# Activations of VectorE's channels half a slot later, and the cosine products inside convolution 1's multiply-adds

## The chip, the cores and the metric

The program runs on one core of a Trainium2 chip. The metric is the device time of one execution in microseconds (us), median of the runs. PE is TensorE, DVE is VectorE, ACT is ScalarE, POOL is GpSimd, SP is SyncE. Each takes its instructions in the order in which the program lists them; semaphores join them.

## The reference

The input x is 8 images of 32 channels, 128 x 128 pixels, f32. `_gn` is a group norm, `_conv` a plain convolution. Cut to what matters:

```python
xb = _patch_match_stack(x)            # per pixel the 8 best of 25 shifts: 256 channels
dct = _conv(xb, dct_w, groups=C)      # "cosine transform": 8 -> 8 in each of 32 groups
h = relu(_conv(_conv(xb, w1), w2, groups=CK, pad=1))   # convolution 1: pointwise, then 3x3 depthwise
h = relu(_conv(_conv(h, w3), w4, groups=CK, pad=1))    # convolution 2
wiener = sigmoid(_conv(_conv(h, w5), w6, groups=CK, pad=1))   # convolution 3
filt = _conv(wiener * dct, inv_dct_w, groups=C)
return _conv(filt, agg_w)
# whole: x = x + L0(_gn(x)); x = x + 5x5 convolution(_gn(x))     (layer 1)
```

## The kernel before

An image is cut into 17 strips of about 8 rows: 136 steps over all images. A step has four slots, numbered by `i` and run in the order 3, 2, 1, 0. Slots 3, 2 and 1 run convolutions 3, 2 and 1, each for another strip, so that a strip goes through convolution 1 in one step, 2 in the next and 3 in the one after; slot 0 ends a strip: the transform's products, the aggregation and the residual sum.

Of the 256 channels, 128 get their depthwise 3x3 on PE (`depthwise_t`, L751) and the other 128 on DVE (`depthwise_v`): one ACT copy with a scale for the first tap (L722) and eight `scalar_tensor_tensor` instructions (L725, "multiply-adds" here) into `acc{i}1`. The activation is an ACT instruction in place (L729 for DVE's channels, L764 for PE's channels). The pointwise products are L670 (`pv`, for DVE's channels) and L694 (`p`, for PE's). Both read the previous convolution's two halves, PE's half `src(0)` first, then DVE's half `src(1)`.

PE, DVE and ACT take their instructions in the order in which this Python code emits them (`manual_schedule`). POOL and SP, which issue DMAs, are ordered by the framework. So the loop over slots is the schedule. In it the generators of a slot are advanced in later places: `depthwise_v` stops at each `yield`. Of a slot's `new_v`, the first `next` emits the copy, the second the eight multiply-adds; the generator is then called `dv` in the next slot and `kept` in the one after.

In slot order, ACT's part of a slot is: the copies of `pv` into `tv` (L678), L722, the two selects of one gather (L616, L617), the copies of `p` into `t` (L701), the copy of the gathered pixels (L638), squares (L452, when there are some), L729, two more selects, two L764. PE's part is: `pv` (slots 3 to 1) or the transform `pc` (L810, slot 0), in slot 3 the aggregation `pa` (L831), then `p`, the gather `pg` (L631), and the depthwise `pw` of the slot before.

The preparation of the next image (differences, squares, the top 8) and layer 1 of the previous one stand in queues; DVE's "D" queue gives out some work in each slot (`tick`), after slot 0's products and before the next multiply-adds. `final_dct` (slot 0) multiplies `acc3` with the transform, four DVE instructions L818 that read PSUM tiles `pc`. In the slot after, `final_add` runs `pa` on PE and then the residual sum L839 on DVE, which frees `pa`'s tile. Layer 1's sum of its products is L936.

All these PSUM tiles (`pv`, `p`, `pg`, `pc`, `pa`, layer 1's `p5` and some small ones) come from one pool of five banks (`ps_x`). A new tile waits for the last reader of the tile that had its bank; which bank it gets is decided when the program is built.

`rows_before_v` moves two rows of `tv` by a DMA on SP (L655), which waits for the multiply-adds that read them.

Of the kernel before, what the change touches and what calls it, by code (L numbers as in the profile page):

```python
# [44 lines left out]
def bm3d_conv_preact(  # L45
# [165 lines left out]
    def push(task):  # L211
        want = next(task, None)
        if want:
            which, cost, *wait = want
            queues[which].append((cost, task, now[0] + (wait[0] if wait else 0)))
# [150 lines left out]
    def prep(b):  # L366

        xn = load_image(b, nc.gpsimd) if b else first
        yield "P", 0
        yield "D", 5.5  # L370
        st = work.tile([P, 8, 6], F32, name=f"st_{b}", tag="st")
        for i in range(8):
            nc.vector.bn_stats(
                st[:, i], xn[:, 3 + 4 * i : 7 + 4 * i, 2 : 2 + W]
            )
        mv = work.tile([P, 2], F32, name=f"mv_{b}", tag="mv")
        nc.vector.bn_aggr(mv, st.rearrange("p a b -> p (a b)"))
        yield "A", 0
        nc.scalar.copy(xn[:, :, 0:2], xn[:, :, 2:3].to_broadcast([P, HR, 2]))
        nc.scalar.copy(  # L380
            xn[:, :, 2 + W :], xn[:, :, 1 + W : 2 + W].to_broadcast([P, HR, 2])
        )
        mr = yield from group_stats(mv, f"a{b}")
        nc.vector.tensor_scalar(
            xn, xn, mr[:, 0:1], mr[:, 1:2], op0=ALU.subtract, op1=ALU.mult
        )
        push(sources(b, xn))

        idx = work.tile([P, 4, 8, K, 4], U32, name=f"idx_{b}", tag="idx", bufs=1)

        sq = dram.tile([NO // 2, 4, HR - 2, HX], F32, name=f"sq_{b}", tag="sq")
        for i in range((HR - 2) // SR):
            pd = ps_d.tile([P, SR // 2, HX], F32, name=f"pd_{b}_{i}", tag="pd")

            for aa in ((2, 4), (0, 0), (1, 1), (3, 2), (4, 3), (5, 5)):
                yield "D", PAIR
                push(squares(b, i, pd, xn, aa, sq, idx))
# [254 lines left out]
    def rows_before_v(i, b, n):  # L652
        v = tv[i - 1]
        if n < NS:
            nc.sync.dma_start(v[:, 0:2], v[:, R : R + 2])  # L655
        else:
            nc.gpsimd.memset(v[:, 0 : i + 1], 0.0)
# [53 lines left out]
    def depthwise_v(i, b, n):  # L711
        v = tv[i - 1]
        nr = R if n < NS else i
        out_ = accp.tile([P, R, W], F32, name=f"acc{i}_{b}_{n}_1", tag=f"acc{i}1")
        acc = out_[:, :nr]
        for k, (dy, dx) in enumerate(
            ((1, 1), (0, 0), (0, 1), (0, 2), (1, 0), (1, 2), (2, 0), (2, 1), (2, 2))
        ):
            tap = dwv[:, i - 1, 3 * dy + dx : 3 * dy + dx + 1]
            rows = v[:, dy : dy + nr, dx : dx + W]  # L720
            if k == 0:
                nc.scalar.activation(acc, rows, AF.Copy, scale=tap)  # L722
                yield out_
            else:
                nc.vector.scalar_tensor_tensor(  # L725
                    acc, rows, tap, acc, op0=ALU.mult, op1=ALU.add
                )
        yield
        nc.scalar.activation(acc, acc, funcs[i - 1])  # L729
        yield  # L730
        rows_before_v(i, b, n)

    def depthwise_t(i, b, n):
# [62 lines left out]
    def final_dct(b, n, acc, xf, j0, j1):  # L796

        for r0 in range(0, R, 4):
            a, z = max(r0, j0), min(r0 + 4, j1)
            if a >= z:  # L800
                continue


            pc = [
                ps_x.tile([P, 4, W], F32, name=f"pc_{b}_{n}_{m}_{r0}", tag="x") for m in range(2)
            ]
            for h in range(2):
                for m in range(2):
                    o = 64 * ((h + m + 1) % 2)
                    nc.tensor.matmul(  # L810
                        pc[m][o : o + 64, : z - a],
                        ldct[64 * h : 64 * h + 64, m],
                        xf[64 * h : 64 * h + 64, m, a:z],
                        start=True,
                        stop=True,
                    )
            for m in range(2):
                nc.vector.tensor_mul(acc[m][:, a:z], acc[m][:, a:z], pc[m][:, : z - a])  # L818
# [179 lines left out]
    def unit(stage, u, *rest):  # L998
        if 0 <= u < len(units) and units[u]:
            if stage is gather_load:  # L1000
                at = (units[u][0], units[u][1] % 8 // 2)
                until(lambda: at in ready, 4.0)
            stage(*units[u], *rest)
# [20 lines left out]
    def turn(credit):  # L1024
        now[0] += 1
        run("D", credit)
        run("A")
        run("P")
        run("Q")

    def until(cond, credit):
        while not cond():
            turn(credit)

    with tc.manual_schedule(engines=ORDERED):
        push(prep(0))
        push(weights())
        push(mixes())
        xbd[0] = dram.tile([P, 2, H, W], F32, name="xbd_0", tag="xbd")
        for i in range(3):  # L1040
            nc.gpsimd.memset(tb[i][0:64, 0], 0.0)
        for u in range(7):
            unit(gather_load, u)

            for _ in range({2: 3, 3: 1}.get(u, 0)):
                turn(4.0)
            unit(gather_select, u - 2)
            unit(gather_pixels, u - 3)
        u = 4

        dt = dv = kept = iter(())

        later = iter(())

        for s in range(len(steps) + 2):
            if s < len(steps):
                b, n = steps[s]
                if s == 2:
                    push(bands())
                if n == (0 if b else 4) and b + 1 < NB:  # L1060
                    until(lambda: b in ready, 4.0)
                    push(prep(b + 1))
                if n == NS - 1 and b + 1 < NB:
                    until(lambda: b + 1 in ready, 4.0)
                    xbd[b + 1] = dram.tile([P, 2, H, W], F32, name=f"xbd_{b+1}", tag="xbd")
            for i in (3, 2, 1, 0):
                si = s - (i - 1 if i else 2)
                live = 0 <= si < len(steps)
                new_v = new_t = iter(())
                if live:  # L1070
                    bi, ni = steps[si]

                if live and i:
                    src = source(i, bi, ni)
                    pointwise_v(i, bi, ni, lws[i - 1], src)
                    new_v, new_t = depthwise_v(i, bi, ni), depthwise_t(i, bi, ni)
                    accs[i, bi, ni] = [None, next(new_v)]
                next(later, None)
                if live and not i:
                    if ni == 0:  # L1080
                        x1d[bi] = dram.tile([C, H, W], F32, name=f"x1d_{bi}", tag="x1d")
                        stats[bi] = work.tile([P, NS + 1, 6], F32, name=f"stat_{bi}", tag="stat")
                    xr, xf, j0, j1 = fins.pop(si)
                run("P")
                if live and not i:
                    final_dct(bi, ni, accs[3, bi, ni], xf, j0, j1)

                run("Q")
                if s < len(steps):
                    unit(gather_select, u + 1, (0,))  # L1090
                    unit(gather_load, u + 3)
                    tick(b, i)
                next(later, None)
                next(new_v, None)
                if live and i:
                    pointwise_t(i, bi, ni, lws[i - 1], src)
                next(kept, None)
                if s < len(steps):
                    unit(gather_pixels, u)
                next(dt, None)  # L1100
                run("A")
                next(dv, None)
                if s < len(steps):
                    unit(gather_select, u + 1, (1,))
                    u += 1
                next(dt, None)
                kept, dv, dt = dv, new_v, new_t
                if live and not i:
                    later = end(bi, ni, xr, j0, j1)
                if not i and 0 <= s - 1 < len(steps):  # L1110
                    fins[s - 1] = final_load(*steps[s - 1])
        next(kept, None)
        for _ in later:
            pass
        until(lambda: {(NB - 1, 0), (NB - 1, 1)} <= done, 4.0)
# [62 lines left out]
```

## Time and profile before

| | |
|---|---|
| median of 3 runs | 6544.47 us (6539.76 to 6554.23) |
| the profiled execution, its own time | 6544.27 us |
| its span in the profile | 6542.5 us |
| PE busy | 6179.8 us (94%) |
| DVE busy | 5857.8 us (90%) |
| ACT busy | 5058.6 us (77%) |
| POOL busy | 3087.2 us (47%) |
| chain that ended last | PE 55%, DVE 26%, POOL 5%, ACT 5%, DMA 4%, issue 4% |

Busy time is the time in which an engine executed. "Idle before" is the time for which an engine stood still ahead of a group of instructions, and the arrow names what ended it. Line numbers are those of the kernel before. Times on a timeline count from the span's start. An image takes about 788 us of the span, and the stalls repeat with it.

### The profile page before, as it was taken

What the parts mean: (1) busy time and instruction counts of PE and PEld (TensorE: products, weight loads), DVE (VectorE), ACT (ScalarE), POOL (GpSimd) and SP (SyncE); (2) the same over time, 40 slices, a digit from 0 to 9 for tenths busy, and PEclk for the clock granted to TensorE, in tenths of its full rate; (3) what the DMA queues carried; (4) which work ended last, traced back from release to release, by engine and by line L of the source; (5) the groups of instructions that cost most, each with busy time, mean ns of one, the idle gap of its engine ahead of it and who ended that gap; (6) DMA issues with size and microseconds to landing.
All of it is one profiled execution on the core that took longest, in us unless ns stands there. A gap on an engine that the chain in (4) does not pass through costs nothing.

```text
span 6542.5 us, 234200 instructions
## 1 busy us (share of the span) xinstructions
PE 6179.8 (94%) x102306; PEld 3215.9 (49%) x102306; DVE 5857.8 (90%) x8828; ACT 5058.6 (77%) x6698; POOL 3087.2 (47%) x5015
## 2 busy tenths in 40 slices
PE   4799999999999999999999999999999999999997
PEld 1444445455554545545454544544545454455553
DVE  7899988999989999999989999889998999878776
ACT  5787769778787877887788787977869788787772
POOL 8345436444364444644446444554345544334334
PEclk8899999999999999999999999999999999999998
DMA  4555555555555555565556555555555555455553
GB/s 85 126 134 144 125 126 143 141 143 138 131 149 138 137 146 129 145 151 134 140 132 156 136 137 141 134 142 140 139 135 134 146 146 138 115 147 144 136 134 81
DMA packets 544960, 886.21 MB, mean 135 GB/s; under 512 B 248880, under 2 KB 312944, under 8 KB 543936
## 3 DMA queue, kind: packets, MB, share of 16 engines
q0 software_dynamic: 383648, 611.87, 37.3%
q1 hardware_dynamic: 157776, 258.11, 16.1%
q8 instruction: 805, 13.19, 0.9%
q10 hardware_dynamic: 2512, 1.25, 0.1%
q14 instruction: 219, 1.79, 0.1%
HBM read 420.60 MB, written 216.49 MB: 97 GB/s over the span
## 4 chain that ended last, share of the span: by engine, by line
PE 55%; DVE 26%; POOL 5%; ACT 5%; DMA 4%; issue 4%; SPq 0%; ACTq 0%; DVEq 0%; POOLq 0%
PE pw L751 18%; DVE acc L725 17%; PE pv L670 14%; PE p L694 13%; PE pg L631 4%; POOL xtd L424 3%; DVE idx L537 3%; PE pc L810 2%; DMA t<-t 2%; DVE df L444 1%; PE pd L459 1%; PE p L924 1%; PE pa L831 1%; DVE acc L818 1%; ACT df L452 1%
## 5 line engine op out<-in xcount | busy, mean ns | idle before, releaser
L725 DVE SCALAR_TENSOR_TENSOR acc<-tv,dwv,acc 128x1024 f32<-128x1024 f32 (+3 forms) x3264 | 4032.1, 1237 | 163.7 <-ACT acc L722 59.9
L751 PE MATMUL pw<-t,dwd 96*32 96x254 f32 (+7 forms) x31680 | 2113.2, 419 | 23.8 <-DMA t<-t 17.9
L751 PEld LDWEIGHTS pw<-t,dwd 96*32 96x32 f32 (+1 forms) x31680 | 1079.9, 110 | 850.1 <-issue 385.5
L616 ACT ACTIVATE sel<-ib,nplace 128x1024 f32<-128x1024 uint8 x1024 | 1170.6, 1143 | 62.3 <-DMA ib<-idxd 62.3
L617 ACT ACTIVATE sel<-sel 128x1024 f32<-128x1024 f32 x1024 | 1086.0, 1061 | 32.5
L670 PE MATMUL pv<-acc,lw 128*32 128x512 f32 x8448 | 964.3, 593 | 49.9 <-DVE acc L818 41.7
L694 PE MATMUL p<-acc,lw 128*32 128x256 f32 x16768 | 977.4, 380 | 19.4 <-DVE xy L936 19.4
L602 POOL DMA_DIRECT2D ib<-idxd x512 | 293.0, 572 | 1209.2 <-ACT sel L616 1099.4
L791 POOL DMA_DIRECT2D xf<-xbd x1088 | 653.6, 633 | 329.2 <-PE pc L810 187.1
L694 PEld LDWEIGHTS p<-acc,lw 128*32 128x32 f32 x16768 | 568.0, 111 | 411.2 <-issue 59.3
L678 ACT COPY tv<-pv 128x512 f32<-128x512 f32 (+2 forms) x784 | 437.0, 578 | 366.9 <-PE pv L670 358.8
L729 ACT ACTIVATE acc<-acc 128x1024 f32<-128x1024 f32 (+3 forms) x408 | 417.3, 1023 | 349.0 <-DVE acc L725 348.8
L631 PE MATMUL pg<-sel,xt 120*32 120x88 f32 (+1 forms) x24576 | 609.9, 245 | 56.6 <-ACT sel L617 56.2
L631 PEld LDWEIGHTS pg<-sel,xt 120*32 120x32 f32 x24576 | 559.3, 111 | 211.5 <-ACT sel L617 72.2
L670 PEld LDWEIGHTS pv<-acc,lw 128*32 128x32 f32 x8448 | 289.1, 111 | 531.8 <-issue 414.6
L764 ACT ACTIVATE acc<-pw 128x512 f32<-128x512 f32 (+2 forms) x808 | 438.7, 573 | 143.6 <-PE pw L751 141.0
L444 DVE TENSOR_TENSOR df<-xn 128x786 f32<-128x786 f32 (+2 forms) x576 | 530.5, 973 | 1.0 <-PE pd L459 0.7
L701 ACT COPY t<-p 128x512 f32<-128x512 f32 x800 | 423.9, 572 | 137.5 <-PE p L694 137.5
L452 ACT ACTIVATE df<-df 128x786 f32<-128x786 f32 (+2 forms) x576 | 457.8, 859 | 40.8 <-DVE df L444 39.5
L722 ACT ACTIVATE acc<-tv,dwv 128x1024 f32<-128x1024 f32 (+3 forms) x408 | 455.1, 1115 | 44.1 <-PE pa L831 29.7
L694 PE MATMUL p<-xb,lw 128*32 128x256 f32 x8192 | 473.5, 383 | 14.4 <-DVE xy L936 14.4
L844 POOL DMA_DIRECT2D x1d<-xr x544 | 278.3, 518 | 417.9 <-DVE xr L839 300.8
(155 smaller groups left out, 6053.2 us busy)
## 6 DMA issues: line engine op xcount, KB each, us to landing
ib<-idxd POOLq DMA_DIRECT2D x512, 256.0 KB, 4.1
xbd<-xb POOLq DMA_DIRECT2D x128, 1024.0 KB, 6.0
xf<-xbd POOLq DMA_DIRECT2D x960, 128.0 KB, 6.8
t<-t SPq DMA_DIRECT2D x792, 128.0 KB
t<-t SPq DMA_DIRECT2D x384, 256.0 KB
tv<-tv SPq DMA_DIRECT2D x384, 130.0 KB
xt<-xtd POOLq DMA_DIRECT2D x240, 180.0 KB, 3.9
xtd<-xl POOLq DMA_DIRECT2D x192, 96.0 KB, 3.3
```

The lines of the kernel that those rows point to most:

```text
L444: nc.vector.tensor_sub(df[:, :, ca:cz], xn[:, r0 : r0 + SR, ca:cz], xn[:, r0 + dy : r0 + dy + SR, ca + dx : cz + dx],)
L452: nc.scalar.activation(df[:, :, ca:cz], df[:, :, ca:cz], AF.Square)
L616: nc.scalar.activation(sel, ib, AF.Square, bias=nplace)
L617: nc.scalar.activation(sel, sel, AF.Relu, scale=-1.0, bias=1.0)
L631: nc.tensor.matmul(pg[C * j : C * (j + 1), :, :, xa:xz], xt[: 8 * QW, f * (NT // 2) + t], sels[j // 2][: 8 * QW, j % 2 * 2 : j % 2 * 2 + 2 ...
L670: nc.tensor.matmul(ps[C * j : C * (j + 1), :hr], lhsT[:, g, P + C * j : P + C * (j + 1)], src(g)[:, h : h + hr], start=g == 0, stop=g == 1,)
L694: nc.tensor.matmul(ps[C * r : C * (r + 1), e, :nb], lhsT[:, g, s], rows[:, r : r + 4 * nb - 3 : 4], start=g == 0, stop=g == 1,)
L722: nc.scalar.activation(acc, rows, AF.Copy, scale=tap)
L725: nc.vector.scalar_tensor_tensor(acc, rows, tap, acc, op0=ALU.mult, op1=ALU.add)
L751: nc.tensor.matmul(pt[u][C * j : C * (j + 1), ka:kz, :nb, xa:xz], dwd[0:hi, i - 1, u, j, dx + 1], t[0:hi, j, ka:kz, :nb, xa + dx : xz + dx ...
L764: nc.scalar.activation(rows[:, u : u + 2 * nh[u] - 1 : 2, :nb], pt[u][:, : nh[u], :nb], funcs[i - 1])
L791: nc.gpsimd.dma_start(xf[p : p + C, m, j0:j1], src[g, m, (h + m + 1) % 2, :, :, ya:yz])
```

## The change

Three edits. In `depthwise_v` the multiply-adds of convolution 1 stop after four of eight and go on in the next slot (slot 0), behind the cosine products L818 and ahead of the D queue's work there. The activation loses the `yield` behind it, so that it is emitted together with `rows_before_v`, two slots after the multiply-adds and ahead of the gather's copy, and no longer one slot after them and behind the squares. The names `kept` and `dv` become `dv` and `made`; the calls after the loop go.

```diff
             else:
+                if i == 1 and k == 5:
+                    yield
                 nc.vector.scalar_tensor_tensor(
                     acc, rows, tap, acc, op0=ALU.mult, op1=ALU.add
                 )
         yield
         nc.scalar.activation(acc, acc, funcs[i - 1])
-        yield
         rows_before_v(i, b, n)
...
                     final_dct(bi, ni, accs[3, bi, ni], xf, j0, j1)
+                if not i:
+                    next(made, None)
 
                 run("Q")
...
                     pointwise_t(i, bi, ni, lws[i - 1], src)
-                next(kept, None)
+                next(dv, None)
                 if s < len(steps):
                     unit(gather_pixels, u)
                 next(dt, None)
                 run("A")
-                next(dv, None)
                 if s < len(steps):
                     unit(gather_select, u + 1, (1,))
                     u += 1
                 next(dt, None)
-                kept, dv, dt = dv, new_v, new_t
+                dv, made, dt = made, new_v, new_t
...
-        next(kept, None)
```

In the built program PE's instructions stand in the same order as before. On ACT, L729 stands in slots 1, 0 and 3 (convolutions 3, 2 and 1) and no longer in slots 2, 1 and 0. On POOL and SP some neighbouring DMAs change places. Of the 3922 PSUM tiles, 196 get a bank whose previous tile is another than before.

More of the change, by code (lines that the diff above doesn't have):

```diff
@@ L1049, in bm3d_conv_preact @@
         u = 4
-        dt = dv = kept = iter(())
+        dt = dv = made = iter(())
         later = iter(())
```

## The prediction

> **What bounds the kernel now.** First the page: who is busy, and which groups wait.
>
> ```profile
> PE 6179.8 (94%) x102306; PEld 3215.9 (49%) x102306; DVE 5857.8 (90%) x8828; ACT 5058.6 (77%) x6698; POOL 3087.2 (47%) x5015
> ...
> L729 ACT ACTIVATE acc<-acc 128x1024 f32<-128x1024 f32 (+3 forms) x408 | 417.3, 1023 | 349.0 <-DVE acc L725 348.8
> ```
>
> PE is the bound, with only 363 us idle in 6542.5, some 115 of them in the first 240 us. ACT stands 349 us in front of L729, but that is no loss by itself: only PE's idle time can come back. So, second, the waits of PE:
>
> ```profile
> PE pg L631 <- ACT sel L617: 56.2, 35, 2.3
> PE pv L670 <- DVE acc L818: 41.7, 20, 3.7
> PE p L694 <- DVE xy L936: 33.7, 18, 3.6
> PE pc L810 <- ACT t L701: 13.9, 7, 3.4
> PE pv L670 <- DVE xr L839: 8.1, 6, 1.5
> PE pc L810 <- DVE acc L818: 5.9, 6, 1.4
> ```
>
> L818 is the second, and no wait names L729: where ACT is late by it, PE mostly doesn't notice. On PE's timeline the stalls repeat with each image, some 25 us in 788. For the image from 3089 to 3877 us: pv<-L818 2.20 (3088.9) and 3.61 (3229.2), pv<-L839 1.42 (3240.9), pg<-sel 1.05, 1.19, 2.18, 2.22, pc<-ACT 1.17 and 1.94, p<-L936 3.02, 0.43 and 2.35, pc<-L818 0.89, and small ones.
>
> Third, one slot 3 in the timeline, ACT then PE: how far ahead of its reader an activation will lie.
>
> ```profile
> 3046.19 1.17 ACT L722 ACTIVATE acc<-tv,dwv 128x1024 f32<-128x1024 f32 x1 [0.32 <-PE pa L831]
> 3047.25 1.14 ACT L616 ACTIVATE sel<-ib,nplace 128x1024 f32<-128x1024 uint8 x1
> 3048.43 1.06 ACT L617 ACTIVATE sel<-sel 128x1024 f32<-128x1024 f32 x1
> 3049.39 1.06 ACT L701 COPY t<-p 128x512 f32<-128x512 f32 x2
> 3050.54 0.59 ACT L638 COPY xb<-pg 128x512 f32<-128x512 f32 x1
> ```
>
> ```profile
> 3045.02 1.04 PE L831 MATMUL pa<-acc,lagg 128*32 128x256 f32 x16
> 3045.89 3.63 PE L694 MATMUL p<-acc,lw 128*32 128x256 f32 x64
> 3049.34 1.14 PE L631 MATMUL pg<-sel,xt 120*32 120x88 f32 x48
> 3050.28 3.63 PE L670 MATMUL pv<-acc,lw 128*32 128x512 f32 x32
> ```
>
> Both chains start at `pa`'s end. ACT runs without a gap from L722 to L701's end at 3050.45; PE is at convolution 2's `pv` at 3050.28.
>
> Fourth, DVE around the products:
>
> ```profile
> 2988.78 2.47 DVE L818 TENSOR_TENSOR acc<-acc,pc 128x512 f32<-128x512 f32 x4
> ...
> 3001.31 0.42 DVE L839 TENSOR_TENSOR xr<-xr,pa 128x256 f32<-128x256 f32 x1 [3.21 <-PE pa L831]
> ```
>
> **Part by part.** The change removes no instruction and adds none. PE's order is the same, so PE can lose only by waits.
>
> *Products earlier.* Four multiply-adds at 1.31 us (eight take 10.52) go behind L818, so L818 may start 5.25 us earlier, but not before its `pc`. At 3088.9 PE waits for it 2.20 us, and the `pv` behind took 5.23 us instead of 3.62. At 3629, pc<-L818 0.89 goes too: 0.9 an image.
>
> But what gets late next? L839 keeps its place, behind all eight multiply-adds, the products and the queue's work, and it frees `pa`'s bank, which the second half of convolution 2's `pv` takes. Around 3229 L818 would free PE 5 us earlier, yet the next stall ends with L839 at 3240.9, and DVE is busy without a gap from 3185 on. PE would wait once, longer, to the same time.
>
> And the new order makes DVE wait. At 2988 `pc` ran from 2987.53; its first half ends at about 2988.6, and the products began right behind it, at 2988.78. Now DVE is through with its four multiply-adds at 2983.5 and stands 5.0 us; behind the products stand the other four, the queue's work and L839. Before, DVE's slack was the 3.21 us in front of L839, where nothing was due. So L839 comes 5.0 - 3.2 = 1.8 us later (2.4 an image on), and DVE has no other gap until 3184. Carried along: L839 at 3143.9 moves to 3145.7 and ends at 3146.1, while PE, 3.2 us earlier by the stall gone at 3089 (2.20 + 1.6 - 2 x 0.3, below), wants that bank at 3142.5; it goes on at 3146.1, 0.4 later than before (3145.7). An image on, the same sum gives 1.0. So the gain at 3089 is lost 57 us later, and the stretch ends with L839 as before, 0.4 to 1.0 late. A stall of over 3 us comes at each of two places, each followed by half clock, up to 1.6 us (next paragraph). I take 2.5 us an image; bounds: -8 (the stalls of 2.20, 3.61 and 1.42 gone, with some half clock) and +5 (1.0 and two or three times 1.6). Near the upper side, since each step is a row of the timeline. It is in six images: +15.
>
> What a stall costs behind itself is in the windows:
>
> ```profile
> 3081.00:3086.50 5.50, 5.50 (x128) 3.23 (x116) 5.36 (x5) 1.23 (x2) 5.50 (x11) 1.00 0.53 121
> 3089.00:3092.20 3.20, 3.20 (x16) 0.70 (x20) 3.06 (x15) 3.17 (x5) 0.58 (x1) 0.50 1.08 239
> ```
>
> (columns: window, length, busy PE, PEld, DVE, ACT, POOL, clock, DMA, GB/s). Behind the stall of 2.20 us the granted clock is 0.50 for 3.2 us, which costs 1.6; behind the ones of 2.18 (3421) and 2.35 (3766) it stays 1.00. [...]
>
> *Activation later: a new wait on PE.* Convolution 1's L729 now stands in slot 3 between L701 and L638; `pv` of convolution 2 reads it in slot 2. L701 ends at 3050.45, instructions overlap by 0.1, L729's median is 1.06: it ends at 3051.41. PE needs it with the ninth of 32 records of `pv`, at 3051.14. With 0.05 to the next matmul (as behind L818 at 3088.9) PE stands 0.3 us. The same subtraction over the timeline gives 0.28 to 0.6 in 80 of 132 steps, about 0.05 in 21, and in 24 nothing, as other matmuls lie between. Behind this wait stands all of PE. About 42 of the 80 lie in DVE's stretches, where the next stall ends by DVE and swallows it; 38 x 0.3 = +11. Bounds: 0 and 80 x 0.45 = 36.
>
> Convolution 2's L729 (slot 0) comes some 4 us ahead of its `pv`, convolution 3's (slot 1) some 5 us ahead of L818: nothing, as long as DVE isn't over 4 us later.
>
> Behind L729 on ACT stand L638, squares, selects and L764. Squares come 1 us later in slots 3, 1 and 0. Matmuls `pd` read them; the slack is 1.1 us with two squares in slot 3, but 0.3 with four, and none at 3393 and 3491. The first is hidden by the stall of 2.18 behind it, the second isn't: +1 an image, +6 (bounds 0 and 15). What ACT no longer waits for DVE brings back pg<-sel 1.05 at 3357 in part (0.3 to 0.7), and a longer L729 ahead of the select at 3377 costs 0.66: nothing together (bounds -7 and +7).
>
> *Banks.* By the two programs, three of the 196 changed ones in each image matter. At 3470 `pc` no longer waits for ACT (1.17) but for L818, which is now early: -1.0, six times -6, with -5.4 for the 0.9 above. At 3555 convolution 2's `p` gets layer 1's bank with its first half and no longer with its second:
>
> ```profile
> 3550.14 1.90 PE L694 MATMUL p<-acc,lw 128*32 128x256 f32 x32
> 3555.06 2.41 PE L694 MATMUL p<-acc,lw 128*32 128x256 f32 x32 [3.02 <-DVE xy L936]
> ```
>
> The 1.9 us that ran ahead of the stall now run behind it: 6 x 1.85 = +11 (0 if DVE gets there earlier, which nothing shows). The third is in the stretch above. At 3766, p<-L936, DVE arrives 0.85 later for its wait in front of the products at 3728: 6 x 0.85 = +5.
>
> *SP and POOL.* L655 keeps its place on SP; its multiply-adds end no later than before apart from the delays above. POOL's swaps are of neighbours at 0.5 to 0.6 us each: taken as nothing (pw<-DMA is 17.9 us in all, the bound on both sides).
>
> **Sum**: +15 +11 +6 +11 +5 -6 -5.4 -1.2 (one pv<-L818 at 5927, DVE not behind later) = +35. On the profiled execution's own 6544.27 (span 6542.5 and 1.8 around it; the median is 6544.47): 6579.
>
> **Rivals.**
> *The stretches loosen (faster).* If L839 were not late when PE wants its bank, stalls of 2.20, 3.61, 1.42, 0.89, 1.17 and 1.05 go, with 2 x 1.6 of half clock: 13.5 an image, 81 in six; less 11 for the new wait: 6474 in full, 6515 at half. For it: ACT's 349 us and L818 as second wait. Against: DVE's unbroken work. It decides at the L839 at 3143.9: if DVE is ready 2 us before PE, it holds.
> *Ends cancel (same).* With the stretch at -2 an image and 3555 at nothing, the sum is -3: 6541.
> *The new wait costs more (slower still).* If PE needs 0.5 us more to get going in all 80 steps, +40: 6620.
>
> **How the numbers follow.** Forecast with its dearer rival 0.66 (0.10 of it the dearer), cancelling 0.15, loosened 0.19. 6579 is the likeliest case. A measurement here can tell about 0.2% (13 us) from no change; all of the first is slower by that. Range 6500 to 6630: it takes in the loosened case at half and the dearer one; the forecast's own is 6560 to 6605.
>
> **What would show it.** Right: a new row pv<-ACT L729 with about 100 waits of 0.3 us; L818 waiting for `pc` with tens of us instead of 16.5, L839's 284.8 down; pv<-L818 small and pv<-L839 grown from 8.1 to 20 or more; p<-L936 up by 10; ACT's wait at L729 nearly gone. Wrong: PE's total idle below 363, or pv<-L839 not grown (the loosened case).

## The result, and the profile after

The changed kernel takes 6577.52 us (median of 6 runs, 6568.42 to 6589.03), the kernel before 6542.99 (6 runs beside them). The ratio is 1.0055, with a 95% interval of 1.0043 to 1.0067: 34.5 us slower. The forecast was 6579.0. The profiled execution of the changed kernel took 6589.03 us (span 6587.3), 44.8 more than the profiled one of before and the slowest of the six; what is read from the two traces below therefore adds up to some 10 us more than the medians show.

Behind the edits the line numbers shift: L725 is now L727, L729 is L731, L810 is L811, L818 is L819, L831 is L832, L839 is L840, L936 is L937. In kernels of the experiments they shift by up to two more.

The page of the changed kernel: busy time by engine, and the group of the products.

```profile
PE 6207.9 (94%) x102306; PEld 3183.9 (48%) x102306; DVE 5851.6 (89%) x8828; ACT 5053.5 (77%) x6698; POOL 3075.0 (47%) x5015
...
L819 DVE TENSOR_TENSOR acc<-acc,pc 128x512 f32<-128x512 f32 (+1 forms) x528 | 321.1, 667 | 239.8 <-PE pc L811 218.5
```

PE's idle time went from 362.7 to 379.4 us, and its busy time, with the same instructions, grew by 28.1. By the clock records of the two traces some 16 of these are half clock: PE was busy for 173 us at a granted clock of 0.50 before, for 206 in this execution. The waits of PE in the changed kernel (us in total, times, longest) show where the order costs:

```profile
PE p L694 <- DVE xy L937: 46.7, 18, 5.2
PE pv L670 <- DVE xr L840: 45.8, 12, 6.0
PE pg L631 <- ACT sel L617: 39.0, 36, 2.3
...
PE pv L670 <- ACT acc L731: 17.1, 24, 1.7
PE pc L811 <- ACT t L701: 15.1, 7, 2.7
```

The wait of `pv` for the products (41.7) is gone from the list, and the one for the residual sum stands there in its place (8.1 before). Layer 1's sum costs 13 us more, the selects 17 less. ACT no longer stands in front of the activation (2.1 us, 348.8 before), but that time did not come to PE: ACT now stands for PE instead, 394.0 us for `pw` (141.0 before) and 493.7 for `pv` (358.8). The waits of DVE show why the residual sum is late, before:

```profile
DVE xr L839 <- PE pa L831: 284.8, 75, 13.8
...
DVE acc L818 <- PE pc L810: 16.5, 14, 4.6
```

and after:

```profile
DVE acc L819 <- PE pc L811: 218.5, 99, 6.9
DVE xr L840 <- PE pa L832: 116.6, 43, 10.7
...
DVE acc L819 <- ACT acc L731: 21.1, 7, 4.0
```

Before, DVE stood in front of the residual sum. It now stands in front of the products. One slot 0 on DVE's timeline, the one that answers to 2988 of before:

```profile
2995.78 5.24 DVE L727 SCALAR_TENSOR_TENSOR acc<-tv,dwv,acc 128x1024 f32<-128x1024 f32 x4
3007.86 2.48 DVE L819 TENSOR_TENSOR acc<-acc,pc 128x512 f32<-128x512 f32 x4 [6.84 <-PE pc L811]
3010.26 5.24 DVE L727 SCALAR_TENSOR_TENSOR acc<-tv,dwv,acc 128x1024 f32<-128x1024 f32 x4
...
3022.34 0.46 DVE L840 TENSOR_TENSOR xr<-xr,pa 128x256 f32<-128x256 f32 x1
```

The 3.21 us of slack in front of the residual sum have become 6.84 us in front of the products, and the sum follows the queue's work without a gap.

The rest hardly shows as a wait. ACT's and PE's timelines in the slot 3 and 2 that answer to 3045 to 3054 of before:

```profile
3068.26 1.06 ACT L701 COPY t<-p 128x512 f32<-128x512 f32 x2
3069.20 1.07 ACT L731 ACTIVATE acc<-acc 128x1024 f32<-128x1024 f32 x1
```

```profile
3069.18 3.93 PE L670 MATMUL pv<-acc,lw 128*32 128x512 f32 x32
3072.92 0.84 PE L459 MATMUL pd<-df,neg 128*32 128x390 f32 x8
```

From `pv`'s start to the next group it was 3.44 us before (3050.28 to 3053.72) and is 3.74 now. The ninth matmul record starts 1.144 us after the first, where it was 0.861. The list of waits holds gaps between modelled ends, 0.2 us the shortest row in it, and names 24 such waits and 17.1 us. Measured by the starts of all whole groups of 32, 101 groups take 0.15 to 1.0 us longer than 3.03 us from first to last start, by 0.33 in the middle and 38.1 us together; before, 6 groups and 2.3 us.

### The profile page after: what moved, and what is told of

The parts are those of the page before. It is cut to its first block, busy times and chain, and to the rows that moved or that the text cites. A ratio compares the mean times of both kernels' runs of the same rounds, so it can differ in the third digit from the quotient of the medians.

```text
span 6587.3 us, 234363 instructions
## 1 busy us (share of the span) xinstructions
PE 6207.9 (94%) x102306; PEld 3183.9 (48%) x102306; DVE 5851.6 (89%) x8828; ACT 5053.5 (77%) x6698; POOL 3075.0 (47%) x5015
## 4 chain that ended last, share of the span: by engine, by line
PE 47%; DVE 28%; ACT 9%; DMA 6%; issue 5%; POOL 5%; SPq 0%; ACTq 0%; DVEq 0%; POOLq 0%
PE pw L752 17%; DVE acc L727 16%; PE pv L670 11%; PE p L694 10%; DVE idx L537 3%; PE pg L631 3%; POOL xtd L424 2%; DVE df L444 2%; ACT sel L616 2%; PE pc L811 2%; DVE acc L819 1%; DMA t<-t 1%; DMA xf<-xbd 1%; ACT acc L731 1%; ACT t L701 1%
## 5 line engine op out<-in xcount | busy, mean ns | idle before, releaser
L727 DVE SCALAR_TENSOR_TENSOR acc<-tv,dwv,acc 128x1024 f32<-128x1024 f32 (+3 forms) x3264 | 4031.4, 1237 | 170.9 <-ACT acc L722 63.7
L752 PE MATMUL pw<-t,dwd 96*32 96x254 f32 (+7 forms) x31680 | 2114.2, 419 | 22.6 <-DMA t<-t 14.1
L670 PE MATMUL pv<-acc,lw 128*32 128x512 f32 x8448 | 983.6, 591 | 73.7 <-DVE xr L840 45.8
L678 ACT COPY tv<-pv 128x512 f32<-128x512 f32 (+2 forms) x784 | 436.2, 578 | 510.7 <-PE pv L670 493.7
L765 ACT ACTIVATE acc<-pw 128x512 f32<-128x512 f32 (+2 forms) x808 | 452.1, 577 | 395.2 <-PE pw L752 394.0
L670 PEld LDWEIGHTS pv<-acc,lw 128*32 128x32 f32 x8448 | 266.1, 110 | 595.6 <-issue 350.8
L819 DVE TENSOR_TENSOR acc<-acc,pc 128x512 f32<-128x512 f32 (+1 forms) x528 | 321.1, 667 | 239.8 <-PE pc L811 218.5
```

Of the source, the lines that this page charges most:

```text
L670: nc.tensor.matmul(ps[C * j : C * (j + 1), :hr], lhsT[:, g, P + C * j : P + C * (j + 1)], src(g)[:, h : h + hr], start=g == 0, stop=g == 1,)
L727: nc.vector.scalar_tensor_tensor(acc, rows, tap, acc, op0=ALU.mult, op1=ALU.add)
L752: nc.tensor.matmul(pt[u][C * j : C * (j + 1), ka:kz, :nb, xa:xz], dwd[0:hi, i - 1, u, j, dx + 1], t[0:hi, j, ka:kz, :nb, xa + dx : xz + dx ...
```

## The experiments

Every median is put against runs of the kernel before on the same chip, whose medians were 6541.83 to 6543.17. The interval of a ratio is 0.08 to 0.17% to each side, some 5 to 11 us: smaller differences are not settled, and steps of that size below are marked.

| kernel | median, us | ratio to before, 95% interval |
|---|---|---|
| changed | 6577.5 | 1.0055 (1.0043 to 1.0067) |
| split alone | 6585.8 | 1.0068 (1.0051 to 1.0085) |
| later activations alone | 6569.6 | 1.0041 (1.0027 to 1.0054) |
| changed, split six and two | 6554.9 | 1.0020 (1.0010 to 1.0030) |
| changed, activation 1 ahead of p's copies | 6556.2 | 1.0018 (1.0009 to 1.0027) |
| later activations alone, activation 1 ahead | 6552.0 | 1.0016 (1.0007 to 1.0025) |
| changed, six and two, activation 1 ahead | 6540.3 | 0.9991 (0.9981 to 1.0000) |
| changed, residual sum early | 6540.4 | 0.9997 (0.9988 to 1.0005) |
| before, residual sum early | 6668.9 | 1.0191 (1.0176 to 1.0206) |
| later activations alone, residual sum early | 6620.5 | 1.0124 (1.0107 to 1.0141) |
| changed, all three, six and two | 6566.3 | 1.0039 (1.0025 to 1.0052) |
| changed, all three, five and three | 6531.0 | 0.9984 (0.9975 to 0.9992) |
| changed, activation 1 ahead, residual sum early | 6524.0 | 0.9973 (0.9964 to 0.9982) |

**The later activations alone.** The changed kernel without the split.

```diff
-                if i == 1 and k == 5:
-                    yield
...
-                if not i:
-                    next(made, None)
```

> The changed kernel without the split: all eight multiply-adds of convolution 1 in one piece ahead of the products, as before; the activations half a slot later as in the change. Theory (the later activation costs its new wait on PE): pv of convolution 2 again takes 3.9 instead of 3.6 us in the ordinary steps, ACT's wait at the activation is gone, pv waits for the products (L818) some 40 us as before, the products' wait for pc stays below 30 and the residual sum's wait for pa near 285; the time is +11 (new wait) +6 (squares) and nothing else: 6560, range 6550 to 6572. Rival A (the loss is all the split's): 6530 to 6545. Rival B (the later activations are the whole loss): 6575 to 6585.

6569.6: inside the theory's range, though 10 above its number, and 26.5 above before. Rival A is out by far; rival B's lower end, 6575, lies within the interval (up to 6578.5), and what speaks against B is the cost of the split alone, next. 105 groups of `pv` are late, by 39.2 us together, and `pv` still waits 41.2 us for the products. What the expectation had forgotten is the bank ahead of layer 1's sum: that wait is 44.2 us here too, against 33.7 before, so the changed bank comes with the activations, not with the split.

**The split alone.** The kernel before, with the second half of the multiply-adds behind the products; all activations at their old places.

```diff
+                if i == 1 and k == 5:
+                    yield
...
+                if not i:
+                    next(dv, None)
```

> The kernel before, with the split alone: convolution 1's second four multiply-adds go behind the products, every activation keeps its old place (convolution 1's still in slot 0, behind the squares). Theory (the split costs by what it makes late, and convolution 1's activation now has to wait for multiply-adds that end 5 to 8 us later in slot 0): ACT's wait at L729 grows from 349 to over 600 us, pv<-L818 falls from 41.7 to below 10, no wait of pv for L729 in the ordinary steps, the products' wait for pc rises from 16.5 to over 150, and the time is 6590 to 6660, slower than the changed kernel. Rival A (the split's own terms are all there is, ACT has room): +15 +11 +5 -12.6 = +18, so 6560. Rival B (the split is the gain and the activations are the loss): 6500 to 6535.

6585.8, 42.7 above before: 4 us under the theory's range, within what the measurement leaves open, and far from both rivals. That it is slower than the changed kernel, as the theory had it, is not settled: the intervals overlap. ACT's wait at the activation doubled, and PE has a new one, for the copies of `pv` that stand behind it on ACT:

```profile
ACT acc L731 <- DVE acc L727: 726.6, 173, 12.3
```

```profile
PE pg L631 <- ACT tv L678: 26.6, 12, 3.7
```

The change's halves do not add: 26.5 and 42.7 alone, 34.5 together. On top of the later activations the split costs only 7.9 us (6577.5 - 6569.6, about the size of the interval); there both of these rows are gone or small (2.1 us, and none), which is the likely reason. In the split alone, six of the new waits are 3.6 to 3.7 us long; at one (3267.9) ACT had stood 12.20 us in front of the activation.

**Convolution 1's activation ahead of the copies of p.** One place earlier on ACT in slot 3, in the changed kernel.

```diff
                 next(new_v, None)
+                if i == 3:
+                    next(dv, None)
                 if live and i:
                     pointwise_t(i, bi, ni, lws[i - 1], src)
```

> The changed kernel with convolution 1's activation one place earlier on ACT: in slot 3 ahead of the two copies of p (L701) and no longer behind them. Theory (PE stands 0.3 us inside convolution 2's pv in most steps because the activation ends 0.3 us too late): the group of 32 pv records of convolution 2 goes back from 3.93 to 3.62 us in the ordinary steps, the row pv<-activation (17.1 us in the changed kernel) is gone, and about 100 x 0.3 us come back less what DVE's stretches swallow: 12 to 30 us below the changed kernel, so 6548 to 6566. Rival (the copies of p, now 1.06 us later, free their banks later, and PE waits for these instead): p or pg waits for L701 by 10 us or more, time within 6 us of the changed kernel or above it.

6556.2: 21.4 back, as the theory said. PE's timeline in the same place:

```profile
3064.16 3.73 PE L670 MATMUL pv<-acc,lw 128*32 128x512 f32 x32
3067.60 0.96 PE L459 MATMUL pd<-df,neg 128*32 128x390 f32 x8
```

Start to start it is 3.44 us again (the 3.73 is an overlapping end of the model), 22 groups are late by 8.8 us together instead of 101 by 38.1, and `pv` waits for the activation 4.8 us instead of 17.1. The rival's new wait for the copies of `p` does not appear.

The same edit in the later activations alone:

> The later activations without the split, and convolution 1's activation ahead of the copies of p. Theory (of the 26.5 us that the later activations cost by themselves, PE's standing inside pv is about 20, the rest is the changed bank ahead of layer 1's sum and the squares): 6569.6 - 21 = 6549, range 6543 to 6556; about 20 groups of pv are late by over 0.15 us instead of 105; p waits for layer 1's sum by some 44 us as without this edit. Rival (the standing is swallowed by waits for the products, which this kernel keeps): 6562 to 6572.

6552.0: 17.6 back. The two together put the price of the new wait at 18 to 21 us, and some 10 us (6552.0 against 6542.1) remain of the later activations.

**Six multiply-adds ahead of the products, two behind.** `k == 5` becomes `k == 7`.

> The changed kernel with the products behind six of the eight multiply-adds and two behind the products, not four and four. Theory (the products come too early for their pc, DVE stands in front of them, and the residual sum is late by it): the products start 2.62 us later; their wait for pc falls from 218 to below 90 us, the wait of pv for the residual sum from 45.8 to below 25, the waits for layer 1's sum from 46.7 to about 42, pv still waits for the products below 10 us; the time falls by 8 to 20 us below the changed kernel: 6558 to 6570. Rival (DVE's standing is harmless, as DVE has slack elsewhere, and the loss is the new wait on PE): within 4 us of the changed kernel.

6554.9: 22.6 under the changed kernel, a little more than the theory's 8 to 20. DVE's wait in front of the products fell to a third,

```profile
DVE acc L819 <- PE pc L811: 71.9, 58, 5.0
```

and `pv`'s wait for the residual sum from 45.8 to 21.2, while 16.9 us of waiting for the products returned (the theory had them below 10). So DVE's standing was not harmless.

Both of these edits together:

> The changed kernel with both single edits that gained: the products behind six multiply-adds (22.6 us under the changed kernel by itself) and convolution 1's activation ahead of the copies of p (21.4 us under it by itself). Theory (two separate losses, one of DVE's standing in front of the products and one of PE's standing inside pv): they add up, 6577.5 - 22.6 - 21.4 = 6533.5, range 6527 to 6541, so some 10 us faster than the kernel before. Rival (PE, freed of one, runs into the other, since both end in DVE's stretches): 6545 to 6555.

6540.3: 37.2 of the 44 us of the sum. That undoes the loss, but the interval of the ratio touches 1: it cannot be called faster than before.

**The residual sum ahead of the queue's work.** In slot 3 it is emitted ahead of what the D queue gives out there, in the changed kernel.

```diff
                     unit(gather_load, u + 3)
-                    tick(b, i)
-                next(later, None)
+                if i == 3:
+                    next(later, None)
+                if s < len(steps):
+                    tick(b, i)
```

> The changed kernel with the residual sum (L840) one place earlier on DVE: ahead of what the D queue gives out in slot 3 and no longer behind it (the work of slot 0's queue and the second four multiply-adds stay ahead of it). Theory (in DVE's unbroken stretches pv waits for the residual sum because queue work stands in front of it): pv<-L840 falls from 45.8 to below 25 us and the time by 5 to 20 us, 6557 to 6573. Rival (DVE now stands at the residual sum, since pa isn't there yet, and the queue's differences come later): the wait of L840 for pa grows from 116.6 to over 200, pd waits for the squares by 10 us more than 28, and the time stays within 5 us of the changed kernel's 6577.5 or goes above it.

6540.4: 37 under the changed kernel, nearly twice the theory's most. `pv`'s wait for the residual sum fell to 8.4 us, as said, and DVE's wait there for `pa` rose to 174.3, short of the rival's 200. Waits for layer 1's sum fell too, from 46.7 in 18 places to 31.9 in 6, and that was not expected: at an image's last strip the generator of the residual sum also puts layer 1 into the queue, and by the move it does so ahead of the queue's work of that slot. So the 37 us are not the residual sum's place alone; no run here parts the two. (The profiled execution of this kernel, 6568.25, is the slowest of its twelve, so its rows are read for their place only.)

With six and two (`k == 7`) and the activation ahead, the same move turns round:

> The two gains together, and the residual sum ahead of the D queue's work in slot 3 as well. Theory: what is left of pv's wait for the residual sum (21.2 us with six and two) falls below 10 and the time is 5 to 10 us under that of the two gains alone. Rival (DVE stands there for pa): same or slower by up to 15 us, the wait of the residual sum for pa above 250.

6566.3, 26 slower than without it. The rival's mechanism was right, and the loss larger than the 15 us that it allowed. DVE stands 299.8 us for `pa`, and PE waits for the products, 33.4 at `pc`, 20.2 at `pv` and 13.9 at `pg`.

With four and four and the activation ahead:

> The changed kernel (four multiply-adds, products, four) with the residual sum ahead of the D queue's work in slot 3 (37 us under the changed kernel by itself) and convolution 1's activation ahead of the copies of p (21 us by itself). Theory (two separate losses of PE): they add up for the most part, as the activation's place did together with six and two (37 of 44): 6577.5 - 37 - 21 = 6519, range 6512 to 6530, faster than the kernel before by some 20 us; about 20 groups of pv late by over 0.15 us, pv<-L840 below 15 us. Rival (as with six and two, DVE stands in front of the residual sum and the products come late for PE): 6545 or more, the wait of the residual sum for pa above 250 us.

6524.0, with a ratio of 0.9973 (0.9964 to 0.9982): the fastest kernel here, 18.8 us faster than before and 53.5 under the changed one, of 58 expected. Its profiled execution (6524.38) lies at the median, and its waits of PE hold these:

```profile
PE p L694 <- DVE xy L937: 33.8, 6, 5.7
...
PE pv L670 <- DVE xr L840: 10.3, 6, 1.8
...
PE pc L811 <- DVE acc L819: 1.4, 3, 0.5
```

Both of DVE's results are now early enough for PE: 11.7 us of waiting for them, where the kernel before had 56. Five multiply-adds ahead and three behind (`k == 6`), with the other two edits:

> Like the kernel with all three edits, with five multiply-adds ahead of the products and three behind. Theory (the early residual sum needs the products early): between four and four (6519 expected) and six and two (6566): 6530 to 6550; PE's waits for the products (pc, pg and pv for L819) between those with four (about none) and with six (67 us). Rival (five and three keeps both gains): below 6520.

6531.0: in the theory's range, nearer to four and four; the 7 us between the two are within the intervals. Waits for the products are 9.7, 8.9 and 6.0 us (`pv`, `pc`, `pg`), 25 in all, where six and two has 67 and four and four 1.4.

Is the early sum a gain of its own? In the kernel before:

> The kernel before with one edit, the residual sum ahead of the D queue's work in slot 3. Theory (the early place pays only with the split, where DVE is through with the products early; without the split it makes DVE stand for pa, and the products, which come last in slot 0's line, come late for PE): the wait of the residual sum for pa goes above 330 us, waits for the products (L818) above 60, time 6550 to 6580. Rival (the early sum is a gain by itself, and has nothing to do with the change): 6505 to 6535.

6668.9: 126 slower, more than even the theory said. The waits of PE for the products:

```profile
PE pc L810 <- DVE acc L818: 59.3, 12, 5.8
PE pv L670 <- DVE acc L818: 56.8, 30, 3.6
...
PE pg L631 <- DVE acc L818: 29.8, 6, 5.0
```

146 us, where before had 48; DVE stands 452.9 us for `pa`. The mean granted clock is 0.967 to 0.971 in these five runs, where before has 0.976 to 0.980 beside them. Which half of the change turns 126 us of loss into 37 of gain?

> The later activations without the split, and the residual sum ahead of the D queue's work in slot 3. The same move of the residual sum cost 126 us in the kernel before and brought 37 us in the changed kernel; this tells which half of the change turned it. Theory (the split: it lets the products come 5 us earlier, and without it DVE, standing for pa, hands them to PE late): as in the kernel before, waits of PE for the products (pc, pv and pg together) above 100 us, DVE's wait for pa above 400, time 6569.6 + 80 to 126 = 6650 to 6696. Rival (the activations: ACT, which stands for DVE's multiply-adds no longer, passes on less of DVE's standing): below 6600.

6620.5, between the theory's range and the rival's. The same move costs 126 us in the kernel before, 51 with the later activations (6620.5 - 6569.6), and brings 37 with the split as well. Added in this order, each half turns some 75 to 90 us of it; the other order, the split alone with the early sum, was not run. With the activations the waits for the products at `pc` and `pv` stay (55.2 and 59.1), but ACT's wait for the multiply-adds (472.9 in the kernel before with the early sum) and `pg`'s 29.8 go; with the split the first two go as well.

## Why the prediction was right

The total was right, and so was the mechanism: what ended the stretches was the residual sum, the activation made PE stand inside `pv`, and a bank moved the run ahead of layer 1's sum. Split into the change's halves, the forecast's terms say +7.4 for the split (+15 +5 -5.4 -6 -1.2) and +28 for the activations (+11 new wait, +11 bank, +6 squares); measured were 7.9 (on top of the activations; alone it is 42.7) and 26.5, each good to some 10 us. Inside the halves, terms were off and made up for each other, so that the total hit its number within 2 us is in part luck. The last column compares the starts of PE's groups in the two profiled executions, place by place, added over six images; the new wait is by experiment.

| step of the prediction | forecast, us | shown, us |
|---|---|---|
| new wait of `pv` for the activation | +11 | +18 to +21 |
| stretches that end with the residual sum | +15 | +15 by themselves, +5 with the new wait in place |
| bank ahead of layer 1's sum (3555) | +11 | +14 |
| later stall there (3766) | +5 | +6 |
| squares ahead of `pd` (3520) | +6 | +6 |
| pg<-sel right behind (3526) | 0 | -5 |
| pg<-sel (3357 and 3377), with the half clock behind | 0 | +4 |
| `pc` no longer behind ACT (3470) | -6 | -9 |
| pc<-L818 gone (3629) | -5.4 | -5.4 |
| pg<-sel (3421) | 0 | -9 |

Together, with the first number for the stretches, the last column gives 35 to 38 us, beside 34.5 by the medians and 44.8 by the two profiled executions.

**The new wait** is the term that was undersized. The forecast had 80 places of 0.3 us, 24 us in all; found were 101 groups, late by 0.33 in the middle and by 38.1 together. It gave 42 of the 80 to DVE's stretches, so that under half would count; but taking 29 to 30 us of the lateness away (38.1 to 8.8, 39.2 to 9.1) brought 18 to 21 us back, so some two thirds of it counted. "A new row with about 100 waits of 0.3 us" misled as a sign, too: the row has 24 waits, and the rest hide in longer groups.

**The stretch** ran as told. Of the gain at 3089 (in the changed trace PE is 2.4 us less behind there, and a further 1.6 after the next group) most is lost 57 us later, at a stall of 1.75 us for the residual sum (the sum's times give 3.6), and the stretch ends with a single one of 5.85 where before had 3.61 and 1.42. The end is 0.1 to 1.8 us later in the six images, 4.5 in all, and not 2.5 in each. The stalls of the first kind are 1.28 to 1.93 us here, and the granted clock is 1.00 over the 6 us behind each of them; over the 6 us behind the second it is 0.55 to 0.73 in the mean (0.72 to 0.77 before, behind the stalls that answer to 3.61). But DVE sets the end of a stretch, so what PE loses to the new wait comes off the stalls there. In the kernel with activation 1 ahead, where the new wait is gone, the first stalls are 1.96 to 2.54 us, four of the six are followed by half clock (0.50 over the 3.3 us from 1567.8), the same places come out 15 us later than before, and the wait for the residual sum is larger than the 45.8 us of the changed kernel:

```profile
PE pv L670 <- DVE xr L840: 54.8, 13, 6.3
```

So the 15 us were right for the stretches by themselves. Windows of the changed kernel behind stalls of 1.75, 1.84 and 2.70 us (window, length, busy PE, PEld, DVE, ACT, POOL, clock, DMA, GB/s):

```profile
3164.60:3168.00 3.40, 3.39 (x44) 1.43 (x48) 3.33 (x4) 3.05 (x5) 3.15 (x6) 1.00 0.15 39
...
3398.10:3401.30 3.20, 3.20 (x74) 2.77 (x75) 3.13 (x3) 3.17 (x6) 2.60 (x5) 0.69 0.64 174
...
3790.70:3793.90 3.20, 3.20 (x44) 1.79 (x48) 3.13 (x4) 1.54 (x2) 3.06 (x2) 0.68 0.10 11
```

Whether half clock follows a stall of about two microseconds is not decided by its length alone: it followed one of 1.84 us here (0.69), and before it did not follow those of 2.18 (3421) and 2.35 (3766), with 1.00 behind both.

**The bank** showed as forecast: at 3555 of before, 32 of the 64 records ran ahead of the stall; now all run behind it, and the stall is 5.04 us where 4.9 (3.02 + 1.9) was told.

```profile
3575.88 5.79 PE L694 MATMUL p<-acc,lw 128*32 128x256 f32 x64 [5.04 <-DVE xy L937]
```

**The squares** cost at `pd` what was told, but the stall for a select right behind, which the prediction left as it was, is shorter by the same. Before and after:

```profile
3520.79 2.75 PE L459 MATMUL pd<-df,neg 128*32 128x393 f32 x14 [0.16 <-ACT df L452]
...
3526.09 1.05 PE L631 MATMUL pg<-sel,xt 120*32 120x88 f32 x41 [2.22 <-ACT sel L617]
```

```profile
3542.15 2.75 PE L459 MATMUL pd<-df,neg 128*32 128x393 f32 x14 [1.11 <-ACT df L452]
...
3546.50 0.99 PE L631 MATMUL pg<-sel,xt 120*32 120x88 f32 x40 [1.27 <-ACT sel L617]
```

**Not foreseen:** the products now wait 21.1 us for convolution 3's activation (seven waits, up to 4.0 us). The prediction had it some 5 us ahead; what these waits cost PE was not measured. And the select at 3421, taken as nothing, brings 9 us. ACT reaches it earlier because the activation no longer stands between it and the squares. Before and after:

```profile
3415.30 3.11 ACT L452 ACTIVATE df<-df 128x786 f32<-128x786 f32 x4
3418.30 1.06 ACT L729 ACTIVATE acc<-acc 128x1024 f32<-128x1024 f32 x1
3419.25 1.15 ACT L616 ACTIVATE sel<-ib,nplace 128x1024 f32<-128x1024 uint8 x1
```

```profile
3437.78 3.11 ACT L452 ACTIVATE df<-df 128x786 f32<-128x786 f32 x4
3440.78 1.14 ACT L616 ACTIVATE sel<-ib,nplace 128x1024 f32<-128x1024 uint8 x1
```

**The rivals.** The loosened case needed DVE to be ready at the residual sum 2 us before PE; in this trace it is 1.75 us behind. Its mechanism was real: with the residual sum taken out from behind the queue's work and the new wait gone, the time fell to 6524, not far from the 6515 of that case at half. It takes two more edits to get there. "Ends cancel" needed nothing at 3555, where 14 us were lost; the dearer new wait needed 0.5 us more in 80 places, 40 us, where the new wait by experiment came to 18 to 21 us in all.

## What to carry to other kernels

An engine that takes its instructions in order should meet, in its list, the result that another engine waits for before the filler that nobody waits for; a step made earlier only pays if what stands behind it in the same list is made earlier as well. Here the split moved the products early and left the residual sum behind the filler, and lost; with the sum ahead of the filler too, 37 us came back, while that same move cost 126 us in the kernel before and 51 with the later activations alone. An activation that frees one engine's wait has to be put where its reader is still at least its own length away (it took 1.07 us here, ended 0.3 us too late in the middle, and that cost 18 to 21 us), and a few tenths of a microsecond on the bounding engine, repeated a hundred times, are looked for in the length of groups, not in the list of waits.

## What the runs showed of the hardware

The granted clock was 0.69 over the 3.2 us behind a stall of PE of 1.84 us, and 1.00 over the 3.4 us behind one of 1.75 (windows above). The length does not decide it: in the kernel with activation 1 ahead, two stalls of 2.54 us at the same place of two images came out differently. The windows behind them (the clock stands third from the end):

```profile
1567.80:1571.10 3.30, 3.30 (x24) 1.04 (x20) 3.23 (x3) 1.81 (x4) 2.77 (x5) 0.50 0.34 101
...
3954.70:3958.10 3.40, 3.40 (x48) 1.35 (x52) 3.33 (x4) 2.80 (x4) 3.26 (x6) 1.00 0.19 49
```

In the changed kernel the stall of 5.04 us at 3575.9 was followed by a mean clock of 0.54 over 4.7 us, so that 64 records of `p` took 5.79 us instead of 3.65. In the stall itself the trace has the clock at 1.00 for the first 2.6 us and at 0.50 for the rest. What sets the moment of the fall was not shown; no run here was made for it.

Most executions of one kernel lie within about 0.2% of its median here (6524.96 to 6547.38 about 6540.3 in twelve runs of one kernel), but a single profiled execution can stand further off: 6568.25 against 6540.4 in the kernel with the residual sum early, 28 us. So no step below some 10 us can be settled by one pair of traces.
